# The start of a fused attention and feed-forward kernel: first norm by square root, first weight rows broadcast before x, two of four stats of the next norm moved

## The chip, the cores and the metric

The kernel runs on one core of one Trainium2 chip. The time is device microseconds (us) of one execution, from the first to the last instruction of the program and what the runtime lays around it; lower is better. A core has five engines that run side by side and wait for each other by semaphores: PE (matrix products; its weight loads are shown as PEld), DVE (vectors), ACT (functions of one operand), POOL (vectors, slower) and SP, which only issues DMAs. ACT and POOL can issue DMAs too. Each engine executes its own instructions in the order in which the program lists them.

## The reference

For x of 2048 tokens (8 x 256) by 512, a layer norm gives xn. An attention branch s works on xn: latent queries, keys and values of width 64, 128 heads of 4 + 64 dimensions, softmax, output product. A feed-forward branch works on the same xn, and its output g, through a silu, scales s before it is added to x. All of it is in fp32.

```python
def _layernorm(x, axis=-1, eps=1e-05):
    m = jnp.mean(x, axis=axis, keepdims=True)
    v = jnp.var(x, axis=axis, keepdims=True)
    return (x - m) / jnp.sqrt(v + eps)
...
        def _qlora_linear(x, wq, A, B):
            w = jnp.tile(wq, (1, 4))
            base = x @ w.T
            lora = x @ A.T @ B.T
            return base + lora * LORA_SCALING
        gate = jax.nn.silu(_qlora_linear(x, w1q, a1, b1))
        up = _qlora_linear(x, w3q, a3, b3)
        return _qlora_linear(gate * up, w2q, a2, b2)
...
    x = L0_attn_x
    xn = _layernorm(x, axis=-1)
    s = _L0_attn_ref(xn, L0_attn_Wq_down, L0_attn_Wq_up, L0_attn_Wq_rope, L0_attn_Wkv_down, L0_attn_Wk_up, L0_attn_Wv_up, L0_attn_Wk_rope, L0_attn_Wo)
    g = _silu(_L0_ffn_ref(xn, L0_ffn_w1q, L0_ffn_a1, L0_ffn_b1, L0_ffn_w3q, L0_ffn_a3, L0_ffn_b3, L0_ffn_w2q, L0_ffn_a2, L0_ffn_b2))
    x = x + s * g
```

The weight of a `_qlora_linear` repeats four times along its input, so the kernel adds the four quarters of xn first and multiplies the sum (128 rows) by the short weight. The low-rank part has rank 2.

## The kernel before

**Two phases.** The first phase (`first_phase`) takes four blocks of 512 tokens: norm, feed-forward branch, and the latent products that attention needs, all but xn's own weights stored to DRAM. The second phase is the attention, two batch rows at a time; the change does not touch it. The schedule is written out by hand: each engine's order is the order of the Python statements.

**One block of the first phase.** `load_x` (L331) loads four tiles `xt` of 128 tokens, from SP, into six rotating buffers. `norm` (L419) takes mean and variance of each tile on DVE (`norm_part`, L411: BN_STATS and BN_AGGR), then the reciprocal root of variance + eps for all four tiles at once: a first guess by a shift of the bits (L428, L430) and three Newton steps of three instructions each (L436 to L438 on DVE for block 0; L440 to L443 on POOL for the others). `norm_one` (L453) applies it, on DVE for block 0. `turn` (L461) transposes the four tiles on PE (16 transposes of 128 x 128 into four PSUM banks, `xpt`) and copies them to `act`, in turn by ACT and DVE for block 0. `sums` (L474) adds the four quarters into `xs` (DVE, one addition on POOL). `narrow` (L494) multiplies by a narrow weight (`pm`), scales the result into `mid` on DVE, stores two rows of it (`low_d`) and loads each back broadcast to 128 partitions (`low`). `down` (L511) is the product `pp` and, on POOL, `sum_x` (L145). `main` (L527) is called six times and handles up to two of eleven chunks of 128 hidden columns at a time: products `px` and `py` on PE, the two low-rank additions with `low` on DVE (L541, L545), silu on ACT, and gate times up into `hT`, two buffers that rotate over three groups of chunks. `fold`, `low_out` and `gate_out` finish the block.

**Row 0 of the weights.** `xs` row 0 is given over to a low-rank term (L505), so the first row of each weight is subtracted from all its other rows. For this, row 0 of w1 and of w3 is broadcast to all partitions. `rows` (L357) holds, at partitions 64 and 65, the row of b13 and the first row of w1, and at 96 and 97 those of w3; three DMAs on ACT's queue bring them. `others` (L364 to L369), written by POOL's memsets, is the two-row weight matrix that spreads them; `spread_first` (L626) multiplies by it on PE, a copy on ACT stores the result in `first`, which borrows the two `hT` buffers. The first eight chunks (two banks per weight, i = 0, 1; k = 0 is w1, k = 1 is w3) are spread at L632, before the first norm; the last three chunks, three small products per weight, in `rest_less_first` (L645), after `down(0)`. `less_first` (L638) subtracts, on POOL for w1 and on DVE for w3; POOL does the rest for both, after `sum_x`. The first `hT` of block 0 (L556) cannot be written before POOL has read `first`.

**Idle transposes.** `warm(count)` (L612) makes PE transpose the identity `count` times into a bank that nobody reads: 26 before the spreads and 2 after.

**Queues.** SP issues, in order: x of block 0, the narrow weights, w_down, w1 and w3 (five pieces each), six small pieces of b13 (`chunk_rows`), x of block 1, and then the stores and loads of block 0. Semaphores of DMAs are reused, so an issue may wait for an earlier transfer. The stats of block 1 stand after the first two calls of `main` (L688).

Of the kernel before, what the change touches and what calls it, by code (L numbers as in the profile page):

```python
# [37 lines left out]
def mla_ffn_gate_kernel(  # L38
# [60 lines left out]
    def bank(name):  # L99
        return ps_all.tile([P, 512], F32, tag="b", name=name)  # L100
# [213 lines left out]
    def first_phase(between):  # L314
# [13 lines left out]
        f2 = pool("f2", 2, st)  # L328
        xts, xns, xnT, xsum, lows = {}, {}, {}, {}, {}

        def load_x(tb):  # L331
            xts[tb] = []
            for n in range(4):
                t = f1.tile([P, D], F32, tag="xt", name=f"xt_{tb}_{n}", bufs=6)
                nc.sync.dma_start(out=t, in_=x[ds(tb * TB + n * P, P), :])
                xts[tb].append(t)

        def by_chunks(to, of):

# [10 lines left out]
        def load_chunks(engine, to, of):  # L350
            for one, two in by_chunks(to, of):
                engine.dma_start(out=one, in_=two)
# [1 line left out]

        rows = f1.tile([P, 3 * TB], F32, tag="h4", name="rows")[:, 0:F]  # L357
        nc.scalar.dma_start(out=rows[64:97:32], in_=b13[0:33:32, :])
        for k, wt in enumerate((w1t, w3t)):
            nc.scalar.dma_start(out=rows[65 + 32 * k : 66 + 32 * k], in_=wt[0:1, :])  # L360
        chunk_rows = f2.tile([P, TB], F32, tag="gs", name="chunk_rows")[:, 0:P]
        nc.gpsimd.memset(chunk_rows[0:32], 0.0)

# [26 lines left out]
        nc.sync.dma_start(out=wdn_sb, in_=w_down.rearrange("(c p) m -> p c m", p=P))  # L390
        for w_sb, wt in ((w1_sb, w1t), (w3_sb, w3t)):
            load_chunks(nc.sync, w_sb, wt)

        of = b13[1:34:32, :].rearrange("k (q f) -> q k f", q=4)
        for n in range(2):
# [5 lines left out]
        for m in range(3):  # L401
# [2 lines left out]
                out=chunk_rows[16 + 2 * m : 18 + 2 * m, 96 : 96 + w],  # L404
                in_=of[3, :, ds(256 + 32 * m, w)],
            )
        load_x(1)

        mvs = {}

# [8 lines left out]
        def norm(tb):  # L419


            for n in range(4):
                norm_part(tb, n)
            mv = mvs[tb]
            ve = f2.tile([P, 4], F32, tag="ve", name=f"ve_{tb}")
            nc.vector.tensor_scalar_add(ve, mv[:, :, 1], EPS)
            i0 = f2.tile([P, 4], I32, tag="i0", name=f"i0_{tb}")
            nc.vector.tensor_single_scalar(i0, ve.bitcast(I32), 1, ALU.logical_shift_right)  # L428
            r0 = f2.tile([P, 4], I32, tag="r0", name=f"r0_{tb}")
            nc.vector.tensor_scalar(r0, i0, -1.0, float(0x5F3759DF), ALU.mult, ALU.add)  # L430
            r = r0.bitcast(F32)
            e = f2.tile([P, 4], F32, tag="e", name=f"e_{tb}")
            for step in range(3):
                new = f2.tile([P, 4], F32, tag=f"r{step}", name=f"r_{tb}_{step}")
                if tb == 0:
                    nc.vector.scalar_tensor_tensor(e, r, -0.5, r, ALU.mult, ALU.mult)  # L436
                    nc.vector.scalar_tensor_tensor(e, e, 1.0, ve, ALU.mult, ALU.mult)
                    nc.vector.scalar_tensor_tensor(new, e, 1.5, r, ALU.add, ALU.mult)  # L438
                else:
                    nc.gpsimd.tensor_mul(e, r, r)  # L440
                    nc.gpsimd.tensor_mul(e, e, ve)
                    nc.gpsimd.tensor_scalar(e, e, -0.5, 1.5, ALU.mult, ALU.add)
                    nc.gpsimd.tensor_mul(new, e, r)  # L443
                r = new

# [168 lines left out]
            for n in range(count):  # L614
                nc.tensor.transpose(idle[:, ds(n % 4 * P, P)], ident, ident)

        warm(26)
        spots = [(slice(0, 3), slice(0, 88)), (slice(0, 2), slice(96, 128)), (slice(2, 3), slice(96, 120))]
        firsts, parts = [], []
        for k in range(2):  # L620
            to = f2.tile([P, 4, TB], F32, tag="hT", name=f"first_{k}")
            to = to.rearrange("p a m -> p (a m)")[:, 0 : NCH * P].rearrange("p (c m) -> p c m", m=P)
            firsts.append(to)
            parts.append(list(by_chunks(to, rows[64 + 32 * k : 66 + 32 * k])))

        def spread_first(k, ps, one, two):  # L626
            nc.tensor.matmul(
# [1 line left out]
            )  # L629
            return one, ps  # L630

        for i in range(2):  # L632
            for k in range(2):
                ps = bank(f"first_{k}_{i}").rearrange("p (q m) -> p q m", q=2)
                nc.scalar.copy(*spread_first(k, ps, *parts[k][i]))
        warm(2)

        def less_first(k, engine):  # L638
            w_sb = (w1_sb, w3_sb)[k]
# [4 lines left out]

        def rest_less_first(k):  # L645
            w_sb = (w1_sb, w3_sb)[k]
            ps = bank(f"first_{k}_2")[:, 0 : 3 * P].rearrange("p (c m) -> p c m", m=P)
            for copy in [
                spread_first(k, ps[:, a, b], *parts[k][2 + i]) for i, (a, b) in enumerate(spots)
            ]:  # L650
                nc.scalar.copy(*copy)
            nc.gpsimd.memset(w_sb[0:1, 8:11], 0.0)
            for a, b in spots:
                one = w_sb[:, 8:11][:, a, b]
                nc.gpsimd.tensor_sub(one, one, firsts[k][:, 8:11][:, a, b])

        stats = norm(0)
        for n in range(4):
            norm_one(0, n, *stats)
        turn(0)  # L660
        sums(0)
        less_first(0, nc.gpsimd)
        narrow(0)
        less_first(1, nc.vector)
# [458 lines left out]
```

## Time and profile before

| | |
|---|---|
| median of 3 runs | 1985.15 us (1983.88 to 1985.93) |
| the profiled execution, its own time | 1985.59 us |
| its span, first to last instruction | 1983.8 us |
| mean granted clock of PE | 0.998 |
| busy: PE, DVE, ACT, POOL | 99%, 79%, 55%, 38% of the span |
| first transpose of x starts | 11.00 us |
| mid starts | 18.78 us |
| first gate (L541) starts | 24.82 us |
| stats of block 1 start | 33.61 us |
| first POOL instruction of block 1's Newton steps | 37.59 us |

The profile is one execution, taken by the hardware. Times count from the start of the span. In a line of the timeline stand the start, the length, the engine, the line of the program, the operation, what it writes and reads, its shape, and how many instructions are merged; in brackets the idle time of the engine before it and what ended it. An engine's name with a q is its sequencer, which waits or issues a DMA. A busy engine is not always at its full rate: PE's clock is granted in shares, and a window of the profile shows the share (1.00 is full, 0.50 is half).

### The profile page before, as it was taken

How to read it: one execution, taken by the hardware profiler on the slowest of the kernel's cores; microseconds unless marked ns; L12 is line 12 of the kernel's file. 1: busy time of each engine (PE TensorE's matmuls, PEld its weight loads, DVE VectorE, ACT ScalarE, POOL GpSimd, SP SyncE). 2: the span in 40 equal slices, each digit the busy share in tenths (PEclk: the TensorE clock that was granted, in tenths of full speed). 3: DMA queues.
4: the chain of work that ended last, by engine and by line, in shares of the span. 5: the costliest groups of instructions: out<-in, count | busy, mean ns of one | idle time of the engine just before them, and what ended most of it. 6: DMA issues, size and time to landing. Idle time of an engine off the chain costs nothing.

```text
span 1983.8 us, 86720 instructions
## 1 busy us (share of the span) xinstructions
PE 1966.9 (99%) x38065; PEld 1401.4 (71%) x38065; DVE 1571.2 (79%) x2666; ACT 1091.4 (55%) x2987; POOL 759.1 (38%) x1113
## 2 busy tenths in 40 slices
PE   8999999999999999999999999999999999999998
PEld 4334577777777767777777767777777767777776
DVE  7764678888787877788787877788787877888788
ACT  3333556556556555556556555556556555556654
POOL 5876545554552323232232323232332323232231
PEclk9999999999999999999999999999999999999999
DMA  6235322222232223221232223221232222222212
GB/s 195 100 118 184 109 88 87 88 69 85 88 129 74 100 87 111 91 87 66 87 117 76 100 87 108 93 88 66 88 115 77 100 87 86 83 88 84 70 56 71
DMA packets 120049, 187.53 MB, mean 95 GB/s; under 512 B 10716, under 2 KB 84844, under 8 KB 119674
## 3 DMA queue, kind: packets, MB, share of 16 engines
q1 hardware_dynamic: 119665, 181.97, 26.8%
q8 instruction: 301, 4.93, 1.0%
q14 instruction: 75, 0.61, 0.1%
q10 hardware_dynamic: 8, 0.02, 0.0%
HBM read 147.86 MB, written 34.10 MB: 92 GB/s over the span
## 4 chain that ended last, share of the span: by engine, by line
PE 91%; POOL 3%; DVE 3%; issue 2%; DMA 1%; ACT 0%; SPq 0%; POOLq 0%; ACTq 0%; DVEq 0%
PE q L173 40%; PE sc L824 34%; PE av L870 11%; PE po L173 2%; PE pf L173 1%; PE qq L249 1%; DVE pt L853 1%; POOL hT L558 1%; POOL h4b L571 0%; DVE nmx L837 0%; POOL h L570 0%; PE py L173 0%; DMA xt<-in_x_dram 0%; PE px L173 0%; POOL h L572 0%
## 5 line engine op out<-in xcount | busy, mean ns | idle before, releaser
L843 ACT ACTIVATE pr<-sc,nmx 128x256 f32<-128x256 f32 x2048 | 814.4, 500 | 471.8 <-DVE nmx L837 469.0
L837 DVE TENSOR_REDUCE nmx<-sc 128x2 f32<-128x512 f32 x1024 | 635.6, 683 | 288.9 <-PE sc L824 264.8
L853 DVE STREAM_TRANSPOSE pt<-pr 128x512 f32<-128x512 f32 x1024 | 635.1, 678 | 0.0
L216 POOL TENSOR_TENSOR e<-e,e 128x256 f32<-128x256 f32 x128 | 93.8, 733 | 1043.8 <-ACT e L211 558.2
L173 PE MATMUL q<-x,ws 128*32 128x256 f32 x8192 | 488.9, 379 | 0.2 <-POOL ws L137 0.2
L824 PE MATMUL sc<-act,qr 32*128 32x256 f32 x8192 | 488.6, 374 | 0.0
L824 PEld LDWEIGHTS sc<-act,qr 32*128 32x128 f32 x8192 | 421.0, 185 | 21.9 <-issue 0.2
L173 PEld LDWEIGHTS q<-x,ws 128*32 128x32 f32 x8192 | 266.1, 110 | 176.3 <-POOL ws L137 0.6
L173 PE MATMUL q<-x,w 128*32 128x256 f32 x6144 | 381.6, 381 | 0.7 <-DVE py L545 0.7
L173 PEld LDWEIGHTS q<-x,w 128*32 128x32 f32 x6144 | 187.0, 110 | 155.8 <-ACT pr L843 35.9
L824 PE MATMUL sc<-kc,qcm 32*128 32x256 f32 x4096 | 280.9, 387 | 0.0
L870 PE MATMUL av<-pt,vpad 128*32 128x128 f32 x8192 | 236.4, 273 | 1.9 <-ACT pr L843 1.2
L870 PEld LDWEIGHTS av<-pt,vpad 128*32 128x32 f32 x8192 | 226.4, 110 | 14.5 <-issue 3.0
L824 PEld LDWEIGHTS sc<-kc,qcm 32*128 32x128 f32 x4096 | 198.2, 184 | 51.9 <-issue 39.4
L211 ACT COPY e<-q 128x256 f32<-128x256 f32 x512 | 202.3, 396 | 25.5 <-PE q L173 25.3
L890 ACT ACTIVATE acc<-av,sides_sb 128x256 f32<-128x256 f32 (+1 forms) x130 | 54.2, 469 | 246.6 <-PE av L870 246.6
L269 POOL TENSOR_TENSOR qcm<-qc,mask_sb 128x1024 f32<-128x1024 f32 x64 | 122.3, 1911 | 0.0
L217 POOL TENSOR_TENSOR e<-e,e 128x256 f32<-128x256 f32 x128 | 93.6, 732 | 10.0
L218 POOL TENSOR_TENSOR qr<-e,e 128x256 f32<-128x256 f32 x128 | 93.6, 731 | 10.1
L310 POOL COPY vpad<-vall 32x128 f32<-32x128 f32 x256 | 74.9, 292 | 10.7 <-PE av L870 2.7
L228 DVE TENSOR_TENSOR qr<-e,q 128x256 f32<-128x256 f32 x128 | 53.9, 421 | 22.5 <-POOL e L216 17.0
L541 DVE SCALAR_TENSOR_TENSOR gate<-low,bcol_sb,px 128x512 f32<-128x512 f32 x44 | 32.8, 745 | 43.6 <-POOL hT L558 24.5
(124 smaller groups left out, 1134.5 us busy)
## 6 DMA issues: line engine op xcount, KB each, us to landing
w<-in_w_rope_dram SPq DMA_DIRECT2D x128, 512.0 KB
ws<-sums_d SPq DMA_DIRECT2D x96, 512.0 KB
sums_d<-ws SPq DMA_DIRECT2D x32, 512.0 KB
x<-xs_d SPq DMA_DIRECT2D x28, 256.0 KB
xt<-in_x_dram SPq DMA_DIRECT2D x16, 256.0 KB
xs_d<-xt SPq DMA_DIRECT2D x16, 256.0 KB
gate_d<-gs SPq DMA_DIRECT2D x16, 256.0 KB
g<-gate_d SPq DMA_DIRECT2D x16, 256.0 KB
```

Source lines behind the costliest of these rows:

```text
L173: nc.tensor.matmul(to[tile_], w[:, tile_], x, start=start, stop=stop, skip_group_check=True)
L211: nc.scalar.copy(self.e[i], self.banks[i])
L216: nc.gpsimd.tensor_add(m6, m6, m1)
L217: nc.gpsimd.tensor_add(m7, m7, m6)
L218: nc.gpsimd.tensor_add(self.out(1, 1), self.split(m7), self.split(m5))
L269: nc.gpsimd.tensor_mul(qcm, qks[b, sg // 2][0].rearrange("p (q i) -> p q i", i=32).unsqueeze(2).to_broadcast([P, 8, 4, 32]), mask_sb[:, ds ...
L310: nc.gpsimd.tensor_copy(vpad[rows, :, :, 8 * t + 4 * (sg % 2) :][..., :4], valls[b][rows, :, sg])
L824: nc.tensor.matmul(sc[r][:, h, :], lhs.rearrange("p t i -> p (t i)"), rhs, start=(part == 0 and h == 0), stop=(part == 2), skip_group_chec ...
L837: nc.vector.tensor_reduce(nmx[:, r, :], scs[n, f][r], AX.X, ALU.max, negate=True)
L843: nc.scalar.activation(p[:, h, :], scs[n, f][r][:, h, :], AF.Exp, bias=nmxs[n, f][:, r, h : h + 1])
L853: nc.vector.transpose(pts[n, f // 2, r].rearrange("p k q i -> p q k i")[:, ds(2 * (f % 2), 2)], prs.pop((n, f, r)).rearrange("p h (k j) -> ...
L870: nc.tensor.matmul(av[32 * r : 32 * r + 32, ds(half * P, P)], vpad[:, k, r, :], pt[r][:, k].rearrange("p q i -> p (q i)"), start=(k == 0), ...
```

## The change

It touches the first 42 us only, in seven places.

1. The rows of w1 and w3 go to two tiles. w1's (with its b13 row) lie in `rows_0` at partitions 64 and 65 and are loaded by two DMAs on ACT's queue, w3's in `rows_1` at 96 and 97, in the buffer of `act1`, loaded by two DMAs on POOL's queue. Both POOL DMAs stand ahead of POOL's memsets.
2. A new [128, 1] tile `one` is set by POOL, and ACT takes its square root, so that the function table of the square root is loaded there.
3. x of block 1 is loaded in two halves: two tiles right after w3, two where all four stood.
4. The norm of block 0 is a square root on ACT (L443 of the new file), a reciprocal on DVE and one Newton step. The other blocks' norm is as it was.
5. 26 idle transposes before the spreads become 6; 2 after them become 14, and these stand after all spreads.
6. The spreads are ordered weight by weight (both banks of w1, then both of w3), and the last three chunks' spreads of both weights stand with them, `spread_rest(0)` before and `spread_rest(1)` after the norm of block 0. The subtractions stay where they were.
7. Stats of block 1: two of the four tiles' stand between `sums(0)` and `narrow(0)`, the other two where all four stood.

```diff
-        def load_x(tb):
-            xts[tb] = []
-            for n in range(4):
+        def load_x(tb, tiles=range(4)):
+            for n in tiles:
                 t = f1.tile([P, D], F32, tag="xt", name=f"xt_{tb}_{n}", bufs=6)
                 nc.sync.dma_start(out=t, in_=x[ds(tb * TB + n * P, P), :])
-                xts[tb].append(t)
+                xts.setdefault(tb, []).append(t)
...
-        rows = f1.tile([P, 3 * TB], F32, tag="h4", name="rows")[:, 0:F]
-        nc.scalar.dma_start(out=rows[64:97:32], in_=b13[0:33:32, :])
-        for k, wt in enumerate((w1t, w3t)):
-            nc.scalar.dma_start(out=rows[65 + 32 * k : 66 + 32 * k], in_=wt[0:1, :])
+        rows = [
+            f1.tile([P, 3 * TB], F32, tag="h4", name="rows_0")[64:66, 0:F],
+            f1.tile([P, KT * TB], F32, tag="act1", name="rows_1")[96:98, 0:F],
+        ]
+        for k, (engine, wt) in enumerate(((nc.scalar, w1t), (nc.gpsimd, w3t))):
+            engine.dma_start(out=rows[k][0:1], in_=b13[32 * k : 32 * k + 1, :])
+            engine.dma_start(out=rows[k][1:2], in_=wt[0:1, :])
+
+        one = f2.tile([P, 1], F32, tag="sq", name="one")
+        nc.gpsimd.memset(one, 1.0)
+        nc.scalar.activation(one, one, AF.Sqrt)
...
             load_chunks(nc.sync, w_sb, wt)
+        load_x(1, range(2))
...
-        load_x(1)
+        load_x(1, range(2, 4))
...
-            for n in range(4):
+            for n in range(2 if tb == 1 else 0, 4):
                 norm_part(tb, n)
...
             nc.vector.tensor_scalar_add(ve, mv[:, :, 1], EPS)
...
+            if tb:
+                i0 = f2.tile([P, 4], I32, tag="i0", name=f"i0_{tb}")
...
+            else:
+                sq = f2.tile([P, 4], F32, tag="i0", name="sq")
+                nc.scalar.activation(sq, ve, AF.Sqrt)
+                r = f2.tile([P, 4], F32, tag="r0", name="r_first")
+                nc.vector.reciprocal(r, sq)
+            for step in range(3 if tb else 1):
...
-        warm(26)
+        warm(6)
...
-            parts.append(list(by_chunks(to, rows[64 + 32 * k : 66 + 32 * k])))
+            parts.append(list(by_chunks(to, rows[k])))
...
-        for i in range(2):
-            for k in range(2):
+        for k in range(2):
+            for i in range(2):
                 ps = bank(f"first_{k}_{i}").rearrange("p (q m) -> p q m", q=2)
                 nc.scalar.copy(*spread_first(k, ps, *parts[k][i]))
-        warm(2)
+
+        def spread_rest(k):
+            ps = bank(f"first_{k}_2")[:, 0 : 3 * P].rearrange("p (c m) -> p c m", m=P)
+            for copy in [
+                spread_first(k, ps[:, a, b], *parts[k][2 + i]) for i, (a, b) in enumerate(spots)
+            ]:
+                nc.scalar.copy(*copy)
...
         def rest_less_first(k):
             w_sb = (w1_sb, w3_sb)[k]
-            ps = bank(f"first_{k}_2")[:, 0 : 3 * P].rearrange("p (c m) -> p c m", m=P)
-            for copy in [
-                spread_first(k, ps[:, a, b], *parts[k][2 + i]) for i, (a, b) in enumerate(spots)
-            ]:
-                nc.scalar.copy(*copy)
             nc.gpsimd.memset(w_sb[0:1, 8:11], 0.0)
...
+        spread_rest(0)
         stats = norm(0)
+        spread_rest(1)
+        warm(14)
         for n in range(4):
             norm_one(0, n, *stats)
         turn(0)
         sums(0)
+        for n in range(2):
+            norm_part(1, n)
         less_first(0, nc.gpsimd)
         narrow(0)
```

More of the change, by code (lines that the diff above doesn't have):

```diff
@@ L426, in norm @@
             nc.vector.tensor_scalar_add(ve, mv[:, :, 1], EPS)
[L427 to L431, printed above, removed]
-            e = f2.tile([P, 4], F32, tag="e", name=f"e_{tb}")
-            for step in range(3):
+            e = f2.tile([P, 4], F32, tag="e", name=f"e_{tb}")
+            if tb:
+                i0 = f2.tile([P, 4], I32, tag="i0", name=f"i0_{tb}")
+                nc.vector.tensor_single_scalar(i0, ve.bitcast(I32), 1, ALU.logical_shift_right)
+                r0 = f2.tile([P, 4], I32, tag="r0", name=f"r0_{tb}")
+                nc.vector.tensor_scalar(r0, i0, -1.0, float(0x5F3759DF), ALU.mult, ALU.add)
+                r = r0.bitcast(F32)
+            else:
[4 more added lines that the diff above has]
+            for step in range(3 if tb else 1):
                 new = f2.tile([P, 4], F32, tag=f"r{step}", name=f"r_{tb}_{step}")
```

## The prediction

> **What bounds the kernel now.** I read the page's busy shares and chain first, then the timeline of the first 24 us, then the windows with the granted clock. The change touches nothing after about 42 us (the last line of the second token block's norm).
>
> ```profile
> PE 1966.9 (99%) x38065; PEld 1401.4 (71%) x38065; DVE 1571.2 (79%) x2666; ACT 1091.4 (55%) x2987; POOL 759.1 (38%) x1113
> ...
> PE 91%; POOL 3%; DVE 3%; issue 2%; DMA 1%; ACT 0%; SPq 0%; POOLq 0%; ACTq 0%; DVEq 0%
> ```
>
> PE carries 91% of the chain; the rest of the chain is the start, where POOL and DVE hand work to PE. A microsecond won or lost there is one of 1984, so the whole start decides about 0.2%.
>
> Of the timeline, PE first (start, length, engine, line, operation, idle before and what ended it):
>
> ```profile
> 1.35 4.96 PE L615 MATMUL idle<-ident 128*128 128x128 f32 x26 [1.35 <-POOL ident masks.py:199]
> 6.24 2.70 PE L627 MATMUL first<-rows,others 2*128 2x512 f32 x8
> 8.87 0.69 PE L615 MATMUL idle<-ident 128*128 128x128 f32 x2
> 11.00 3.68 PE L467 MATMUL xpt<-ident,xt 128*128 128x128 f32 x16 [1.45 <-DVE xt L459]
> ...
> 22.07 1.62 PE L627 MATMUL first<-rows,others 2*128 2x264 f32 x12
> ```
>
> then POOL and DVE:
>
> ```profile
> 1.24 0.20 POOL L362 MEMSET chunk_rows<- 32x128 f32 x1
> ...
> 2.56 0.09 POOL L369 MEMSET others<- 1x1 f32 x1
> ...
> 8.02 0.17 DVE L426 TENSOR_SCALAR ve<-mv 128x4 f32<-128x4 f32 x1
> ...
> 10.40 1.92 DVE L459 TENSOR_SCALAR xt<-xt,mv,r 128x512 f32<-128x512 f32 x4
> ...
> 17.38 0.69 DVE L481 TENSOR_TENSOR xs<-xs,xs 128x512 f32<-128x512 f32 x1 [1.17 <-POOL xs L480]
> 18.78 0.75 DVE L497 TENSOR_SCALAR mid<-pm,cks_sb 128x512 f32<-128x512 f32 x1 [0.70 <-PE pm L173]
> ...
> 24.82 0.75 DVE L541 SCALAR_TENSOR_TENSOR gate<-low,bcol_sb,px 128x512 f32<-128x512 f32 x1 [1.55 <-PE px L173]
> ...
> 28.58 1.28 DVE L556 TENSOR_TENSOR hT<-gate,py 128x512 f32<-128x512 f32 x2 [0.50 <-POOL w_sb L655]
> ...
> 33.61 0.69 DVE L416 BATCH_NORM_STATS2 st<-xt 128x6 f32<-128x512 f32 x1
> ```
>
> and two windows (stretch, its length, busy time and instructions of PE, PE's loads, DVE, ACT, POOL, then the granted clock and the DMA):
>
> ```profile
> 5.30:8.70 3.40, 3.40 (x17) 1.91 (x15) 2.21 (x8) 1.22 (x3) 0.65 (x5) 1.00 1.08 294
> 8.70:15.50 6.80, 5.35 (x31) 4.00 (x34) 4.69 (x15) 2.10 (x4) 1.14 (x7) 0.50 0.56 144
> ```
>
> Three things are to be seen. The norm's square root is 2.38 us of DVE (8.02 to 10.40). The first gate (L541) is named as waiting for PE's px, but that began at 23.61 and is only 0.43 us of matmul per bank; the trace's semaphore updates give the last piece of `low` at 24.39, so the gate waits for mid, then low_d, then low. And the two windows at the bottom: from 5.30 to 8.70 PE was busy without a break, but after 6.3 only with the spreads, which use two rows of the array; the clock then fell to half. Transposes ran at half clock (16 in 3.68 us; less the last one's own 0.42, 0.22 us apart). At full clock they are 0.11 us apart (at 44.54, 8 in 1.09, less 0.27).
>
> [...] eight spreads, alternating between rows 64 and 96, took 2.63 us up to the next matmul, while a 512-wide one alone takes 0.45 us (pp: 32 in four strips side by side, 3.61/8), which would be 3.6 us. [...] no POOL DMA is in this trace. [...]
>
> **The change part by part**, against the profiled execution of 1985.59 us (span 1983.8, the rest around it).
>
> *Start of the spreads.* They wait for `others`, the rows and 6 idle transposes (done by 2.7). `others` took POOL 1.41 us, 1.24 to 2.65; two POOL DMAs and one memset (0.1) now stand ahead. [...] 1.24+2.1+1.41, about 4.8. The ACT rows come at 4.61 in the semaphore record, no later now. So 4.8 us against 6.24; range 4.6 to 6.8.
>
> *The spreads themselves.* Before, 26 transposes opened the clock at 5.29 and two row groups alternated. Now 6 transposes (1.3 us) are too few for a window, so the spreads run at half clock: 0.88 us each, not 0.44. The loop is now by k first, so the four of one row group come one after another; the second group starts when the first one's last is issued: (3+4) x 0.88, about 6.1 us. The remaining 12 small ones took 1.62 at full clock, 3.2 at half; some 1.3 lies beside the last big ones. Sum about 7.9: they end near 12.7. With the clock open it would be about 4.0. Bounds: 4.0 (open from the first) to 10.2 (half clock, nothing side by side: 8 x 0.88 + 3.2).
>
> *The norm.* ACT's sqrt, DVE's reciprocal and one Newton step (3) replace 2+9 small DVE instructions at 0.2 us: 11 become 4, and one hand-over each way. About 1.2 us against 2.38. But the sqrt stands in ACT's queue behind the three copies of the first rest, which wait for PE's spreads (done about 11.4): sqrt near 12.1, xt normed from 13.2 to 15.1, instead of 10.40 to 12.32. Behind the waiting copies and sqrt, DVE waits for the reciprocal. The first table load moves to a time when ACT is idle, and the second (Silu, 24.32) was there before: nothing. If the cover by PE's lateness were gone, the norm would be 1.2 us earlier.
>
> *Transposes.* PE goes from 12.7 through 14 idle transposes and 16 real ones, 30 in all. At half clock 30 x 0.213 would be 6.4; once a window with enough of them ends, the rest run at 0.107. In before a window 45% full of transposes (8.70 to 12.12) did not open it and the next did. Taking 60% as needed and a random phase, it opens 3.7 us after 12.7 on average, after 17 or 18; 12 more take 1.3. End about 17.8, against 14.68: +3.1. By phase 16.9 to 19.1. No transfer hides this: xs, pm, POOL's weight subtractions and the stores all start from `act`.
>
> *Half of the next norm.* Two pairs of stats move from 33.61 (0.80 a pair, 1.6 saved) to between the sums and mid. DVE reaches them at 17.38+0.69+3.1=21.2 and leaves at 22.95; pm ends at 18.70+2.7=21.4, so mid begins at 23.0, +4.2, that is 1.1 beyond the shift. Queued behind: mid, low_d, both low loads, the gate. The x tiles for it are issued right after w3 (10.74 before), six small DMAs earlier than the 14.30 of before, and land before 21 us; chunk_rows, used at 22.06, was landed at 14.9 and moves back by two issues of 0.4.
>
> *The rests after pp.* 1.62 us of PE between pp and px goes away, but px does not set the gate; low does. Nothing.
>
> *Sum.* First gate +4.2. The hT at 28.58 had waited 0.50 for POOL to free the `first` buffer; POOL is late by 3.1, DVE by 4.2, so that wait is absorbed: +3.7. The norm in the old place is 1.6 shorter: +2.1 from there on. From 38 us the chain is DVE and POOL again and passes this on. 1985.59+2.1=1987.7; the median shown lies 0.44 lower: **1987.3**.
>
> **Rivals.** *A, as summed* (spreads cold, start near 4.8): 1986.0 to 1989.0 by the phase of the window. For it: the half clock after a window of spreads. Against: one window is thin evidence.
>
> *B, the same with a late start*: [...] `others` at 6.8, everything 2 us later: +4.1, about 1989.5. [...] Against: ACT's and SP's issues are 0.25 to 0.6 us.
>
> *C, faster*: the clock is open while the spreads run, or becomes so soon. Then they end near 8.8, 14 idle ones near 10.4, sqrt at 8.4, xt 9.4 to 11.3, transposes end at 12.0: -2.7. Mid loses 1.1, the hT wait of 0.5 goes, the stats give 1.6: -3.7, about 1982. It decides by when the spreads end: the sum above is zero where the transposes end 1.0 late, at 15.7, which needs the spreads done by about 10.5. For it: nothing showed how a window weighs two-row work beside idle time. Against: 8.70.
>
> *D, the change doesn't do what it says*: the gains of norm and stats are met by the late spreads, 1985.2, plus or minus 0.7.
>
> **How the numbers follow.** A 0.46, B 0.28, C 0.18, D 0.08. The bound of 0.2% (about what a measurement of this kernel can tell from no change) is 4 us: above 1989.1 or below 1981.2. Slower holds two thirds of B and an eighth of A, 0.26; faster under half of C, 0.08; within it 0.66. The time is A's, 1987.3; A's own range is 1986.0 to 1989.0. To leave out no more than 2 in 10 it must take in D, half of C and most of B: 1983.0 to 1990.2.
>
> **What would show it.** In the profile after: the spreads' start (4.8) and end (12.7), the granted clock under them (0.5), the last xpt (17.8), the first gate (29), the last small DVE instruction before the third gate pair (39.6, 37.42 before). A spread phase of 4 us, or a clock of 1.0 under it, makes A wrong; so does mid waiting for PE instead of the stats. If transposes end by 15.7, C holds.

## The result, and the profile after

The kernel after takes 1988.59 us (median of 22 runs, 1986.54 to 1991.18), the kernel before, on the same chip, 1985.18 us. The ratio is 1.0018 with a 95% interval of 1.0011 to 1.0024: 3.4 us slower. Its profiled execution took 1989.78 us (span 1988.0), 4.2 us over that of the kernel before.

Busy shares and chain of the page after, the same two lines as before:

```profile
PE 1969.7 (99%) x38057; PEld 1408.8 (71%) x38057; DVE 1569.5 (79%) x2659; ACT 1092.5 (55%) x2989; POOL 760.9 (38%) x1116
...
PE 93%; DVE 3%; POOL 2%; issue 1%; ACT 0%; DMA 0%; POOLq 0%; ACTq 0%; SPq 0%; DVEq 0%
```

DVE has seven instructions fewer; nothing else of note moves here. The story is in the timeline. PE first (start, length, engine, line, operation, idle before and what ended it):

```profile
1.36 1.54 PE L628 MATMUL idle<-ident 128*128 128x128 f32 x6 [1.36 <-POOL ident masks.py:199]
3.80 7.63 PE L640 MATMUL first<-rows,others 2*128 2x512 f32 x20 [0.90 <-POOL others L375]
11.36 3.25 PE L628 MATMUL idle<-ident 128*128 128x128 f32 x14
14.40 2.96 PE L480 MATMUL xpt<-ident,xt 128*128 128x128 f32 x16
17.28 3.66 PE L173 MATMUL pm<-act,ck_sb 128*32 128x256 f32 x64
```

The spreads start 2.4 us earlier than before (3.80 against 6.24) but last 7.63 us; the last transpose of x ends at 17.36 (14.68 before). That PE ran at half clock is read from durations: 14 idle transposes in 3.25 us are 0.22 us apart (3.25 less the last one's own 0.42, by 13), as at half clock before. The granted clock's record has its first entry at 16.53 us (to full), and where it has no entry a window shows 1.00, which is not evidence of full speed.

Then ACT, where the square root stands behind copies of spreads:

```profile
10.38 0.58 ACT L655 COPY first<-first 128x264 f32<-128x264 f32 x3
10.83 0.24 ACT L443 ACTIVATE sq<-ve 128x4 f32<-128x4 f32 x1
```

and DVE:

```profile
11.10 0.18 DVE L445 RECIPROCAL r_first<-sq 128x4 f32<-128x4 f32 x1 [2.85 <-ACT sq L443]
...
20.66 0.69 DVE L423 BATCH_NORM_STATS2 st<-xt 128x6 f32<-128x512 f32 x1
...
22.28 0.72 DVE L510 TENSOR_SCALAR mid<-pm,cks_sb 128x512 f32<-128x512 f32 x1
...
28.05 0.75 DVE L554 SCALAR_TENSOR_TENSOR gate<-low,bcol_sb,px 128x512 f32<-128x512 f32 x1 [2.11 <-DMA low<-low_d]
...
31.24 1.29 DVE L569 TENSOR_TENSOR hT<-gate,py 128x512 f32<-128x512 f32 x2 [0.45 <-POOL w_sb L669]
...
38.49 0.74 DVE L554 SCALAR_TENSOR_TENSOR gate<-low,bcol_sb,px 128x512 f32<-128x512 f32 x1
```

DVE waits 2.85 us for the square root. mid is 3.50 us later than before, the first gate 3.23, the first hT 2.66. The "third gate pair" below is the two gate instructions of the third call of `main`, DVE's first work after its part of block 1's norm; the pair starts at 38.49, 37.42 before, only 1.07 later. So two thirds of the delay at the start are made good by 38 us. But the whole is 4.2 us longer.

To see where the rest comes from, the same matmul is found in two traces, and its start in one is taken from its start in the other; this difference is called the shift. The table has it for all runs (us against the profile before; "near 100" is near 100 us of the profile before; the last two columns compare runs of each kernel with runs of the kernel before on the same chip):

| run | third gate pair | near 100 | near 180 | near 1900 | median minus before's | ratio, 95% interval |
|---|---|---|---|---|---|---|
| after | 1.07 | 2.01 | 2.63 | 4.30 | 3.41 | 1.0018, 1.0011 to 1.0024 |
| after_again | 1.52 | 2.19 | 3.37 | 5.49 | 3.17 | 1.0016, 1.0009 to 1.0022 |
| e1_no_idle | 0.31 | 1.47 | 3.65 | 5.26 | 3.84 | 1.0017, 1.0011 to 1.0024 |
| e2_whole_stats | 3.29 | 4.13 | 4.97 | 6.40 | 5.28 | 1.0026, 1.0018 to 1.0034 |
| e6_alternate | 1.35 | 1.98 | 2.95 | 3.37 | 3.22 | 1.0014, 1.0007 to 1.0020 |
| e3_sqrt | 3.12 | 3.90 | 5.09 | 4.61 | 2.07 | 1.0010, 1.0004 to 1.0017 |
| e4_half_stats | -1.52 | -1.70 | -1.77 | -2.38 | -1.02 | 0.9996, 0.9988 to 1.0005 |
| e5_spread_part | 2.49 | 2.33 | 3.08 | 3.70 | 3.69 | 1.0021, 1.0014 to 1.0027 |
| e7_sqrt_stats | -1.19 | -0.45 | -0.21 | -0.10 | 0.60 | 1.0006, 0.9998 to 1.0014 |
| e8_count | -0.04 | 0.58 | 1.64 | 2.26 | 1.64 | 1.0008, 1.0000 to 1.0016 |
| e9_sqrt_first | -4.3 | -3.65 | -3.33 | -3.75 | -1.46 | 0.9990, 0.9984 to 0.9997 |
| e10_rows_act | 2.67 | 3.48 | 3.86 | 5.74 | 5.52 | 1.0026, 1.0014 to 1.0037 |
| e12_warm26 | -0.3 | 0.04 | -0.61 | -0.56 | 1.53 | 1.0005, 0.9997 to 1.0013 |

One profile is one execution: between executions the start moves with the clock (it opened at 16.53 and 17.40 us in the two profiles of the kernel after) and with the rows (w3's came at 6.05 to 6.6 us from POOL's queue), so the first columns tell where a microsecond is lost, the last ones how much on average. Both profiles of the kernel after are of executions slower than its median (by 1.2 and 1.6 us), that of e3_sqrt is its slowest of 21, and that of e4_half_stats its fastest of 13.

### The profile page after: what moved, and what is told of

Same layout as the page of the kernel before. It is cut to its first block, busy times and chain, and to the rows that moved or that the text cites. A ratio compares the mean times of both kernels' runs of the same rounds, so it can differ in the third digit from the quotient of the medians.

```text
span 1988.0 us, 86704 instructions
## 1 busy us (share of the span) xinstructions
PE 1969.7 (99%) x38057; PEld 1408.8 (71%) x38057; DVE 1569.5 (79%) x2659; ACT 1092.5 (55%) x2989; POOL 760.9 (38%) x1116
## 4 chain that ended last, share of the span: by engine, by line
PE 93%; DVE 3%; POOL 2%; issue 1%; ACT 0%; DMA 0%; POOLq 0%; ACTq 0%; SPq 0%; DVEq 0%
PE q L173 40%; PE sc L843 34%; PE av L889 11%; PE po L173 2%; PE pf L173 1%; PE py L173 1%; PE px L173 1%; PE qq L249 1%; DVE pt L872 1%; POOL h4b L584 0%; DVE nmx L856 0%; POOL h L583 0%; POOL hT L571 0%; PE first L640 0%; PE pm L173 0%
```

## The experiments

**The change taken apart.** Two runs take one part out of the kernel after, with the kernel after once more beside them.

> The kernel after, unchanged, as a control. It has two questions. (1) Theory: the +1.07 us at the third gate pair (38.49 us against 37.42) comes from the start and repeats within 0.1 us. (2) Theory: the further growth of the shift (+2.0 us at 76.5, +2.7 at 180, +4.2 at the end) is chance of this one execution (the landing of low_d of the second block took 0.9 us longer): the third gate pair again near 38.5, but the shift at 76 us only +1.1, and the drift over the last 1800 us of either sign. Rival: the growth belongs to the program (queues moved by the start), and then +2.0 at 76.5 and +2.7 at 180 come again. Ratio to the kernel before: theory 1.0005 to 1.0015, rival 1.0018 or more.

The third gate pair came at 38.94, 0.45 later than in the first profile (the clock opened at 17.40, not 16.53, so pm came later): the start repeats within half a microsecond, not 0.1. The shift near 100 us was +2.2 again, close to the rival's number, and the growth after 60 us is the program's. The ratio, 1.0016, fell between what the two had said.

`e2_whole_stats`, the stats move undone:

```diff
-        load_x(1, range(2))
...
-        load_x(1, range(2, 4))
+        load_x(1)
...
-            for n in range(2 if tb == 1 else 0, 4):
+            for n in range(4):
...
-        for n in range(2):
-            norm_part(1, n)
```

> The kernel after with the statistics of the second block back in one place (all four tiles in its norm, the four loads of x after the small rows). Theory, as in the prediction: moving them saves 1.6 us at the old place and costs up to 1.1 us in front of mid, so undoing it makes mid earlier by 0 to 1.1 us (21.2 to 22.3) and the third gate pair later by 0.5 to 1.6 us (39.0 to 40.1 against 38.49), total +0.5 to +1.6 us. Rival: the two pairs of statistics hold mid, low_d and the gate up by more than they save; then the first gate comes over 1.6 us earlier (below 26.4) and the total falls.

Median 1991.50 us against 1989.39 for the kernel after beside it on the same chip: 2.1 us worse, above the theory's upper end, and so is the third gate pair (40.71). DVE's timeline of that run:

```profile
21.52 0.75 DVE L509 TENSOR_SCALAR mid<-pm,cks_sb 128x512 f32<-128x512 f32 x1 [0.27 <-PE pm L173]
...
27.47 0.75 DVE L553 SCALAR_TENSOR_TENSOR gate<-low,bcol_sb,px 128x512 f32<-128x512 f32 x1 [2.26 <-DMA low<-low_d]
...
31.87 1.28 DVE L568 TENSOR_TENSOR hT<-gate,py 128x512 f32<-128x512 f32 x2 [1.67 <-POOL w_sb L668]
...
40.71 0.74 DVE L553 SCALAR_TENSOR_TENSOR gate<-low,bcol_sb,px 128x512 f32<-128x512 f32 x1
```

mid and the gate are earlier without the stats in front (21.52 and 27.47), but hT then waits 1.67 us for POOL, which still has to free the `first` buffer. In the kernel after this wait is 0.45. From the first hT to the third gate pair it is 8.84 us here and 7.25 in the kernel after: the 1.6 us of stats. The other 0.6 us at the third gate pair lies ahead of hT; the start of this execution was late (transposes of x end at 17.86, not 17.36). So the stats in front of mid stood in time in which DVE would have waited for POOL anyway: they cost nothing, and all of the 1.6 us at the old place is gain.

Then each part alone, in the kernel before:

`e3_sqrt`, the norm by square root with the early load of its table (1.28 us, at 4.25 here and at 1.52 in the kernel after):

```diff
+        one = f2.tile([P, 1], F32, tag="sq", name="one")
+        nc.gpsimd.memset(one, 1.0)
+        nc.scalar.activation(one, one, AF.Sqrt)
...
+                nc.scalar.activation(sq, ve, AF.Sqrt)
+                nc.vector.reciprocal(r, sq)
-            for step in range(3):
+            for step in range(3 if tb else 1):
```

`e4_half_stats`, the split of `load_x(1)` and of the stats:

```diff
+        load_x(1, range(2))
-        load_x(1)
+        load_x(1, range(2, 4))
...
+        for n in range(2):
+            norm_part(1, n)
```

`e5_spread_part`, the rest of the change (with the rows in two tiles on two queues):

```diff
-        warm(26)
+        warm(6)
-        for i in range(2):
-            for k in range(2):
+        for k in range(2):
+            for i in range(2):
...
+        spread_rest(0)
         stats = norm(0)
+        spread_rest(1)
+        warm(14)
```

`e7_sqrt_stats` is the first two together.

> The kernel before with only the norm changed (first tokens by square root on ScalarE, reciprocal and one Newton step, with its early table load). Theory: seven fewer small DVE instructions and one hand-over each way; xt normed 1.2 us earlier (9.2 to 11.1 instead of 10.40 to 12.32), transposes of x 1.2 us earlier if the clock lets them, first gate about 23.7 instead of 24.82, third gate pair 36.3 instead of 37.42, total -1.1 us. Rival: earlier transposes fall into the half-clocked window (8.70 to 15.5) and pm with them, so pm runs longer at half clock and the first gate is not earlier: 0. Second rival: the square root waits behind the copies of the spreads in ScalarE's queue, and the norm is no earlier: 0.

> The kernel before with only the statistics of the second block split (two of the four x tiles loaded ahead of the small rows and their statistics taken between the sums and mid). Theory: 1.6 us saved at the old place, at most 0.9 us lost in front of mid (mid at 18.78 waits 0.70 us for pm, so 0.7 of the 1.6 us hides there), third gate pair 36.5 instead of 37.42, total -0.9 us (bounds -1.6 and 0). Rival: the early loads of x delay the small rows, and the statistics hold mid and the gate: total 0 to +1.

> The kernel before with only the broadcast part of the change (first rows on two queues in two tiles, 6 idle transposes instead of 26, all twenty spreads ahead of x by k first, 14 idle ones). Theory: this part carries all of the loss; the transposes of x end at 17.4 as in the kernel after, since the norm (DVE only) is ready at about 12.3 and PE is not before 14.4; first gate about 27.7 (no statistics in front of mid), third gate pair about 39.9 (37.42 + 2.7), total +2.5 us against the kernel before, more than the whole change. Rival: the loss comes from the statistics or from the square root waiting in ScalarE's queue; then this part alone is within 1 us of the kernel before.

> The kernel before with the square root and the split statistics, but its own broadcast. Theory: the two gains add, third gate pair about 35.4 to 36 instead of 37.42, total -1.5 to -2 us against the kernel before, and so faster than both. Rival: both gains are the same slack (mid then waits for pm behind the clock), and the total is that of the better one alone, -1 us.

The spread part alone gives +3.7 us, as much as the whole change loses, and 1.2 us above the theory's 2.5; its third gate pair, 39.91, is where the theory had it. That the other two parts together come to little is taken up below. Half of the stats alone gives -1.0 us on the median (its interval holds no change) and -1.52 at the third gate pair, near the better of the expected bounds. The square root alone is *slower* by 2.1 us: the theory is out; its second rival has the mechanism (below), not the size. The two together are +0.6 us (the interval holds no change), where the theory had said -1.5 to -2 and its rival -1: both are out. DVE's timeline with the spread part alone:

```profile
20.71 0.75 DVE L500 TENSOR_SCALAR mid<-pm,cks_sb 128x512 f32<-128x512 f32 x1 [0.34 <-PE pm L173]
...
31.07 1.29 DVE L559 TENSOR_TENSOR hT<-gate,py 128x512 f32<-128x512 f32 x2 [1.57 <-POOL w_sb L659]
...
39.91 0.74 DVE L544 SCALAR_TENSOR_TENSOR gate<-low,bcol_sb,px 128x512 f32<-128x512 f32 x1
```

Again hT waits for POOL, 1.57 us: the late `act` delays DVE and POOL alike (mid by 1.93 us against before, POOL's first addition for `xs`, 1.79 us in the profile before where DVE's took 0.69, by 2.32), and it is POOL's work that ends last ahead of hT.

**Why the square root did not pay.** ACT's timeline of e7_sqrt_stats, in which the variance was ready near 7.0 us:

```profile
5.20 0.20 ACT L362 ACTIVATE one<-one 128x1 f32<-128x1 f32 x1
7.83 2.05 ACT L644 COPY first<-first 128x512 f32<-128x512 f32 x4 [2.43 <-PE first L636]
9.74 0.24 ACT L439 ACTIVATE sq<-ve 128x4 f32<-128x4 f32 x1
```

The square root stands behind four copies that wait for PE's spreads, and these for the rows of w3. xt was normed from 10.81, later than with the eleven small DVE instructions (10.40 before, 10.31 in e4_half_stats). In e3_sqrt's own profile the rows of w3 came late as well, the spreads went on from 8.32 at half clock, and the square root ran only at 12.48. The order explains why nothing was gained; 0.4 us in e7_sqrt_stats is not the 2.1 us that e3_sqrt lost on the median, and the rest is taken up with e8_count. The remedy is an order; `e9_sqrt_first` is e7_sqrt_stats with the norm's statements ahead of the spreads:

```diff
+        stats = norm(0)
         for i in range(2):
             for k in range(2):
                 ps = bank(f"first_{k}_{i}").rearrange("p (q m) -> p q m", q=2)
                 nc.scalar.copy(*spread_first(k, ps, *parts[k][i]))
...
-        stats = norm(0)
```

> The kernel before with the square root and half of the statistics, its own broadcast, and the norm of the first tokens placed ahead of the broadcast's four copies in ScalarE's queue. Theory: the square root gained nothing in this place because it stood behind those copies (it ran at 9.74 us, when the variance was there at about 7.0); ahead of them it runs at 8.0 to 8.3 us, xt is normed from 9.2 to 9.4 instead of 10.81, the transposes of x (at half clock) end near 13.5 instead of 15.1, first gate 24.4 to 24.8 instead of 25.84, third gate pair near 35.0 instead of 36.23, total -1.2 us against the one with the square root behind the copies, about -0.6 us against the kernel before, and near that with half of the statistics alone. Rival: the copies, now 1 to 2 us later, hold the weight subtraction on POOL and so hT; or the clock's half window takes the gain (pm longer): no change.

```profile
7.66 0.20 ACT L439 ACTIVATE sq<-ve 128x4 f32<-128x4 f32 x1 [2.20 <-DVE ve L429]
7.77 0.57 ACT L645 COPY first<-first 128x512 f32<-128x512 f32 x1
9.05 1.57 ACT L645 COPY first<-first 128x512 f32<-128x512 f32 x3 [0.72 <-PE first L636]
```

The square root runs at 7.66, xt is normed from 8.71, and the median is 1984.42 us: ratio to before 0.9990 (0.9984 to 0.9997), 1.5 us under the kernel before, and the one version here whose interval lies below it. How much of that is the square root is not settled: half of the stats alone gave -1.0 us, and the two intervals overlap. The profile shows -3.75 us, more than the median, and its clock did not fall to half again at the start (16 transposes of x in 1.91 us, 0.11 apart; windows below). Of the 21 executions three show a mean clock of 1.000, at 1981.8 to 1982.0 us; the other 18 show 0.997 to 0.999, at 1983.1 to 1986.4.

**What spaces the spreads.** Three runs on the kernel after. `e6_alternate`:

```diff
-        for k in range(2):
-            for i in range(2):
+        for i in range(2):
+            for k in range(2):
```

`e10_rows_act`, the same and all rows on ACT's queue:

```diff
-        for k, (engine, wt) in enumerate(((nc.scalar, w1t), (nc.gpsimd, w3t))):
+        for k, (engine, wt) in enumerate(((nc.scalar, w1t), (nc.scalar, w3t))):
```

`e12_warm26`:

```diff
-        warm(6)
+        warm(26)
```

> The kernel after with the eight big spreads in the order of the kernel before (row group 64 and row group 96 in turn, i outside and k inside). Theory: at half clock 0.88 us each, two groups side by side; the eight take 3.5 us instead of about 6, so the spreads end near 9 instead of 11.3, the square root comes near 9 instead of 10.8, the transposes of x end near 15.5 instead of 17.36, first gate near 26.2, total -1.8 us. Rival 1: the copies on ScalarE (0.57 to 0.7 us for 1024 columns each) and the two row groups are not what spaces them, only the clock is: the same end near 11.3 and no change of the total (within 0.3 us). Rival 2: the clock opens under alternated spreads; then they end near 8.

> The kernel after with the big spreads in turn (as in the run with alternated groups) and the W3 rows on ScalarE's queue behind the W1 rows instead of POOL's. Theory: in the run with alternated groups the W3 group waited for its rows until 6.05 us and then needed 5.3 us by itself at half clock, so the spreads ended at 11.39 in spite of the order; from ScalarE's queue the rows land earlier (4.6 to 5.2 us, as in the kernel before) and the spreads end near 10.0 to 10.5; square root near 9.7, transposes of x end 0.9 to 1.3 us earlier if the clock's window falls as before, total -1 us against the kernel after. Rival: the fourth transfer on ScalarE's queue lands no earlier than 6 us (each issue 0.25 us, and the landing about 2 us or more after it); then the end stays at 11.4 and the total within 0.3 us.

> The kernel after with 26 idle transposes instead of 6 at its start. Theory: they last until about 6.2 us and open the clock for one window, so the spreads begin 2.2 us later but run at full clock (0.43 us each, two groups) for up to 3.4 us; they end near 10.5 (11.3 in the kernel after), then the clock falls to half for the rest of the start; transposes of x end near 16.5 to 17, total -0.5 us against the kernel after. Rival 1: a window full of two-row matmuls does keep the clock open; then the transposes run at full clock and end near 14, total -3 us. Rival 2: the late start costs more than the clock gives: spreads end after 11.5, total +0.5 us.

Alternating changed nothing (spreads end at 11.39 against 11.43; median 3.2 us above before's, as for the kernel after beside it): the first weight load of the w3 group (the spreads of w3, on rows 96 and 97) came at 6.05 us, right after PE's sequencer had ended a wait at 6.03, although PE's queue was free for it near 5.2; this is read as the landing of its rows. In the kernel after, in its own order, it came at 6.09. With the rows on ACT's queue it got worse, median 1991.40 us, 5.5 above before's; PE's timeline:

```profile
4.26 2.04 PE L640 MATMUL first<-rows,others 2*128 2x512 f32 x2 [1.37 <-DMA rows<-in_w1t_dram]
8.29 5.30 PE L640 MATMUL first<-rows,others 2*128 2x512 f32 x18 [1.98 <-DMA rows<-in_w3t_dram]
13.52 3.25 PE L628 MATMUL idle<-ident 128*128 128x128 f32 x14
```

The w3 rows landed at about 8.26. ACT's issue record shows the delay: the third and fourth transfers were issued only at 3.18 and 4.15 us, after the first and second had landed (their last packets moved at 2.64 and 3.50), while the kernel after issues its w3 rows from POOL at 1.47 and 2.19. The kernel before has the same fault: its third transfer, the w3 row, was issued at 3.68 and moved its last packet at 6.12, 2.4 us later (w1's: 1.87, 4.11 and 2.2), and its first w3 spread came at 6.90; in the other profiles with its broadcast it came at 7.0 to 7.2 (e4_half_stats, e7_sqrt_stats) or at 7.9 to 8.4 (e3_sqrt, e8_count, e9_sqrt_first). So the second queue does what it is for: the w3 rows come 0.3 to 2.3 us earlier (6.05 to 6.6 against 6.9 to 8.4). After that the w3 group needs 5.3 us at half clock, and that is what the kernel after pays for.

With 26 idle transposes the median is 1987.41 us, 1.5 us above before's on the same chip, where the kernel after stood 3.4 and 3.2 us above it: 1.6 to 1.9 us better, by medians from different chips; the theory had said 0.5. PE's timeline and three windows (stretch, its length, busy time and instructions of PE, PE's loads, DVE, ACT, POOL, the granted clock, DMA):

```profile
1.36 4.64 PE L628 MATMUL idle<-ident 128*128 128x128 f32 x26 [1.36 <-POOL ident masks.py:199]
5.94 4.32 PE L640 MATMUL first<-rows,others 2*128 2x512 f32 x20
10.19 3.25 PE L628 MATMUL idle<-ident 128*128 128x128 f32 x14
13.23 2.73 PE L480 MATMUL xpt<-ident,xt 128*128 128x128 f32 x16
```

```profile
4.66:8.07 3.41, 3.41 (x22) 2.48 (x21) 2.55 (x7) 0.70 (x2) 0.50 (x4) 1.00 1.10 302
8.07:11.49 3.42, 3.42 (x19) 3.15 (x17) 1.24 (x7) 2.60 (x10) 1.66 (x11) 0.50 1.11 294
11.49:14.90 3.41, 3.41 (x18) 3.41 (x17) 1.36 (x3) 0.57 (x1) 0.00 (x0) 0.50 0.63 195
```

The spreads start 2.1 us later and end 1.2 us earlier (10.26); the clock also opens 1.6 us earlier than in the first profile of the kernel after (14.90, not 16.53). PE is busy without a break in all three windows, yet the clock falls after the first, which held ten idle transposes and then spreads; it opens again at 14.90, after a window full of transposes. The first rival (two-row work keeps the clock) is out. The profile is of an execution faster than its median (1984.94 against 1987.41 us).

`e1_no_idle` drops `warm(14)`:

> The kernel after without the 14 idle transposes between the spreads and the transposes of x. Theory: they stand in PE's queue ahead of the 16 real ones and last until 14.4 us, when xt has been ready since 12.4; without them the transposes of x start at 12.4 and run at half clock (0.22 us each, 3.6 us), end 15.9 to 16.1 instead of 17.36, first gate 1.3 us earlier (26.7), total -1.3 us against the kernel after. Rival: the idle ones keep PE busy and so open the clock; without them the clock stays half through pm and pp, which then take up to 3.6 us longer between them, and the first gate is not earlier (28 or later), total 0 or +2.

Both were half right. The transposes started at 12.91, when xt was ready, and ended at 16.58; but the clock opened only at 18.32 and pm took 4.53 us, not 3.66. The third gate pair is 0.8 us earlier than in the first profile of the kernel after and 1.2 earlier than in the second, and the median is not lower (1990.06 against 1989.39): a gain at the start that does not arrive. Most of it is lost between 145 and 180 us in this profile (shift 1.66, then 3.65); why stays open.

**Where the shift grows after 60 us.** SP's timeline in the second block, before:

```profile
62.05 0.53 SPq L499 DMA_DIRECT2D low_d<-mid  x1
63.72 0.80 SPq L503 DMA_DIRECT2D low<-low_d  x2
```

and after:

```profile
63.26 0.53 SPq L512 DMA_DIRECT2D low_d<-mid  x1
65.84 0.80 SPq L516 DMA_DIRECT2D low<-low_d  x2
```

The store of two rows of mid must land before it is read back; from issue to issue that took 1.67 us before and 2.58 us after. Of the ten profiles of before and of the table down to e7, the three without the square root have a gap of 1.67, the seven with it 2.3 to 2.6. The list of DMA queues has two of kind "instruction" (q8 and q14), and in the second group an 8 KB packet of q14 moves ahead of the store's second 2 KB packet, which starts within 0.02 us of that packet's end in all seven: after, at 64.43 (first row), 64.45 (instructions, for 0.61 us) and 65.05 (second row); before, the rows went at 63.22 and 63.26 and the instructions at 63.62. So it might be only how long the instruction streams are. (The packet makes up 0.6 of the 0.9 us; the other 0.3 us lies between the second row and the next issue, and its cause was not found.) `e8_count` is the kernel before with three instructions that nobody needs:

```diff
+        one = f2.tile([P, 1], F32, tag="sq", name="one")
+        nc.gpsimd.memset(one, 1.0)
+        nc.scalar.copy(one, one)
+        nc.scalar.copy(one, one)
```

> The kernel before with three tiny instructions that nobody needs (one memset of a 128x1 tile on POOL and two copies of it on ScalarE), so that the instruction streams of these two engines are as long as in the kernels with the square root; the norm is that of before. Of nine profiles, the six with the square root show low_d of the second token block read back 2.3 to 2.6 us after its issue, the three without (before, half of the statistics, spread part) 1.67 us; an 8 KB instruction fetch moves 1.2 us after that issue in the first group, 1.5 to 1.6 us in the second, and low_d's own packets move at 1.17 us. Theory: the length of the streams shifts the fetch onto low_d's packets; here too the fetch then comes 1.2 us after the issue and the gap is 2.3 to 2.6 us, and the shift against the kernel before grows by 0.6 to 0.9 us between 60 and 100 us. Rival: the square root's side effects or chance made it; the gap stays 1.67 us. Total +0.3 to +0.9 us by the theory, 0 by the rival.

```profile
62.17 0.53 SPq L503 DMA_DIRECT2D low_d<-mid  x1
64.59 0.80 SPq L507 DMA_DIRECT2D low<-low_d  x2
```

The gap is 2.42 us, the instruction packet moves at 63.37 between the rows at 63.33 and 63.91, and the shift grows from -0.02 near 60 us to +0.58 near 100. The theory holds for the gap. By 180 us the shift is +1.64, and the median is 1.64 us above before's (ratio 1.0008, 1.0000 to 1.0016), more than the theory's 0.9: three idle instructions, with no loss at the third gate pair (-0.04), cost about as much as the kernel after loses between 60 and 180 us (1.6 us). Whether the later 1 us of it comes from instruction packets too was not tried, nor was it which engine's stream it is (both were lengthened).

This bears on the square root, whose kernels all have such instructions (`one`) and the long gap. An estimate from the medians: e7_sqrt_stats lies 1.6 us above e4_half_stats, and e3_sqrt, less the 1.64 of e8_count, keeps about 0.4 us, which is how much later e7_sqrt_stats normed xt. In the whole change, 3.7 for the spreads (e5_spread_part) less 2.1 for the stats (e2_whole_stats) plus 1.6 makes 3.2, where 3.4 and 3.2 were measured. So most of what the square root lost seems to be the shifted instruction stream, not the order on ACT. The intervals reach 1.2 to 1.8 us to either side, so this is not shown.

## Why the prediction was right, and where its sum was not

The likeliest case (spreads at half clock, start near 4.8, 1986.0 to 1989.0) was the one that happened, and the measured 1988.59 us lies in its range. The forecast of 1987.3 is 1.3 us short, by errors of both signs. The half clock, the path from spreads to gate and the late third gate pair were foreseen; that the sum ended so near was in part luck.

- **Start of the spreads: 4.8 said, 3.80 found** (4.23 in after_again), below its bounds. The term that failed is that of the two POOL issues, 2.1 us with a memset, which no trace had shown: they took 0.72 and 0.49.
- **Length: 7.9 said, 7.63 found, half clock as said** (0.85 us from one big spread to the next of its group: 4.81, 5.66). But a reading behind it failed: that the rows lay ready at 4.61. The w3 rows landed at 6.05 to 6.6 here, and at 6.9 or later in the kernel before. The sum came out because the order of the loop put the second group at about that time as well; e6_alternate shows that the order was worth nothing. Half clock under the spreads cost 1.6 to 1.9 us, as far as e12_warm26 shows it.
- **Norm behind the first rest's copies: right in kind** (square root said 12.1, found 10.83, for the spreads ended 1.3 us earlier than said). In the kernel after it is hidden, since PE is busy until 14.4. That the square root would save 1.2 us without that cover is wrong in this program's order (+2.1 us alone); ahead of the copies xt is normed 1.7 us earlier than before (8.71 against 10.40), but what this is worth in the total is not settled.
- **Transposes: 17.8 said, 17.36 found; mid 23.0 and 22.28; first gate 29 and 28.05.** All carry the earlier end of the spreads, but only in part: the clock was to open 3.7 us after that end, by the estimate that a window 60% full of transposes is enough (one 45% full had not opened it), and opened 5.1 us after it (5.9 in after_again, where a window with 12 of 16 possible transposes did not open it). In the sum for mid, 22.95 should read 22.8 (21.2 and two pairs of 0.80).
- **The wait of hT: the step that failed.** The text said that the wait for POOL is absorbed as DVE is later than POOL. It remained (0.45), and without the moved stats it would have grown to 1.67. So the stats' 1.1 us in front of mid were no cost; their move is worth 1.6 us in the profiles and 2.1 by the medians (e2_whole_stats), not 0.5.
- **Third gate pair: +2.1 said, +1.07 and +1.52 found** in two profiles.
- **"From 38 us the chain passes this on": failed.** It grew by 0.7 to 0.9 us in the second block, through the read-back of `low_d`, and by 0.6 to 1.2 us up to 180 us. No term of the sum had this; without it 1985.18 and 1.07 to 1.52 would give 1986.3 to 1986.7, under the forecast. Beyond 180 us both profiles of the kernel after grow by another 1.7 and 2.1 us, in small steps, mostly at score matmuls, while those with the broadcast of before do not (-0.6 to +0.6 us) and others with the new one do in part (0.1 to 1.9); the medians ask for less than 1 us of it. Its cause was not found.

Of the rivals, B failed by its late start (others at 6.8, which no trace had shown), C by the half clock. D had the right kind, a gain by stats against a loss by the spreads, but not the balance: the gain is smaller (2.1 against 3.7 us), and 1988.59 lies outside its range.

## What to carry to other kernels

Moving work ahead is worth what the engine does with it there: the second queue brought the rows 0.3 to 2.3 us earlier, and PE, at half clock after only six idle transposes, spent it on slow spreads. A short result that others wait for must stand ahead of waiting work in its engine's queue: with half of the stats moved in both, the square root behind four copies gave +0.6 us and ahead of them -1.5 us. And price a delay in front of one engine by who is waited for next: here DVE had 1.7 us to give away, because hT waited for POOL. Last, a difference of 1 to 2 us in 1985 may come from a few instructions that do nothing (three made 1.64 us in e8_count): a run that adds only those belongs beside it.

## What the runs showed of the hardware

**In these profiles two-row matmuls did not open the clock, and did not hold it after seven or ten transposes.** In the profile before the clock changed at 5.29, 8.70 and 15.53 us, 3.41 and twice 3.41 us apart. In the kernel after one such window of 3.41 us, counted back from 16.53, held nothing but spreads; its 1.00 is the missing entry:

```profile
6.29:9.70 3.41, 3.41 (x13) 2.53 (x12) 1.82 (x5) 1.37 (x3) 1.28 (x8) 1.00 1.14 296
```

PE was busy throughout, and the transposes after it still ran at half speed (0.22 us apart, above); in e1_no_idle two such windows in a row (4.67 to 11.50) left it so, and it opened at 18.32. (The window of the prediction, 5.30 to 8.70, began with seven transposes and lost the clock; that of e12_warm26, 4.66 to 8.07, with ten, and lost it too.) Whether this is due to the two rows or to something else about these matmuls was not tried. Counted in such windows: at half speed, windows with up to 13 transposes and no other matmuls than spreads (after_again, e4_half_stats, e8_count) did not open it, those with 15 or 16 did (16 in the kernel after, 13.12 to 16.53); at full speed a window with ten (e12_warm26) lost it, and one with eleven kept it (e9_sqrt_first, one profile):

```profile
4.46:7.87 3.41, 2.50 (x15) 1.50 (x13) 2.68 (x7) 1.20 (x4) 0.37 (x2) 1.00 1.09 289
7.87:11.29 3.42, 3.37 (x20) 2.19 (x21) 2.84 (x9) 2.60 (x5) 1.76 (x9) 1.00 1.12 306
```

PE was busy for only 2.50 us in the first of these windows and kept its clock, where 3.41 us with more two-row work and one transpose less lost it.

**Packets of instructions held up a data transfer.** In these traces instructions have queues apart from data (q8 with 301 packets and q14 with 75 on the page before; which engine's they are is not shown). Where an 8 KB packet of q14 moved between the two 2 KB rows of a store, it took 0.44 to 0.65 us, and the second row started as it ended, 0.4 to 0.6 us late (65.05 in the kernel after, the first at 64.43; 63.22 and 63.26 before). In the profile of e8_count, three instructions more were enough for it to fall on a transfer that is waited for (packet at 63.37, rows at 63.33 and 63.91).
